# Experts on sorted tokens: 200 indirect transfers per image in place of dense expert products

## The chip, the cores and the metric

The kernel runs on one core of a Trainium2 chip. The time is the device time of one execution in microseconds (us), as the median of several executions. A profile is one further execution with every instruction recorded. Engines are named as in the profile: PE (TensorE, matmuls; PEld its weight loads), DVE (VectorE), ACT (ScalarE), POOL (GpSimd), SP (SyncE, which here only issues DMA transfers). Each engine works through its own instructions in program order and waits on semaphores of the others.

## The reference

Four images of 32 x 128 x 128 pass two layers. Layer 0 is an attention over blocks of channels; it enters here only as the work that layer 1 is interleaved with. Layer 1 turns the image into 4,096 rows ("tokens") of 128 numbers each (the sizes B, N in the functions below are not used), adds a linear attention, and then a mixture of experts:

```python
def _L1_ffn_ref(x, router_w, router_b, expert_w, expert_b):
    B, N, D, C, E, K = (8, 8192, 128, 128, 8, 2)
    router_probs = jax.nn.softmax(x @ router_w + router_b, axis=-1)
    top_p, top_i = jax.lax.top_k(router_probs, K)
    top_p = top_p / jnp.sum(top_p, axis=-1, keepdims=True)
    expert_out = jnp.einsum('bnd,edc->bnec', x, expert_w) + expert_b
    gathered = jnp.take_along_axis(expert_out, top_i[..., None], axis=2)
    return jnp.einsum('bnk,bnkc->bnc', top_p, gathered)
# ...
t = t + _L1_attn_ref(_ln_t(t), L1_attn_Wk, L1_attn_Wq, L1_attn_Wv)
t = t + _L1_ffn_ref(_ln_t(t), L1_ffn_router_w, L1_ffn_router_b, L1_ffn_expert_w, L1_ffn_expert_b)
```

Of the eight expert results of a token only the two with the highest router probability count. A kernel may compute all eight and weight six of them by zero, or compute two.

## The kernel before

The program is a loop over images. While the attention of image b is emitted, generators ("streams") are advanced between its instructions: the preparation of image b + 1 and layer 1 of image b - 1. A stream gets a begin, an end and a number of steps, in per cent of the attention's own units (`UNITS`); each `yield` of a generator is a step.

```python
    UNITS = 3 * NJ * NJ * NCH * (NCH - 1) // 2 + 5 * NJ * NCH
# ...
    for b in range(B):

        streams = list(carried)
        carried = []
        if b == 0:
            for kc, begin, end in ((1, 0, 5), (2, 6, 20), (3, 25, 45)):
                streams.append((prep(0, kc, states[0]), begin, end, 10))
            streams.append((setup_weights(), 50, 60, 4))
        else:
            streams.append((layer1(b - 1, states[b - 1], False), 7, 97, 161))
        if b + 1 < B:
            nxt = states[b + 1]
            streams.append((prep(b + 1, 0, nxt), 66, 84, 10))
            streams.append((prep(b + 1, 1, nxt), 85, 99, 10))
            carried.append((prep(b + 1, 2, nxt), 2, 20, 10))
            carried.append((prep(b + 1, 3, nxt), 30, 50, 10))
        done = [0] * len(streams)
        start = clock[0]
        for _ in attend(b, states[b]):
            t = 100 * (clock[0] - start) / UNITS
            for n, (steps, begin, end, count) in enumerate(streams):
                while t >= begin and done[n] * (end - begin) < (t - begin) * count:
                    next(steps, None)
                    done[n] += 1
        for steps, *_ in streams:
            for _ in steps:
                pass
    finish_late()
    last = states[B - 1]
    for _ in layer1(B - 1, last, True):
        pass
```

So layer 1 of images 0, 1 and 2 lies inside the attention of images 1, 2 and 3, and layer 1 of the last image stands alone at the end (`alone`). The attention itself, for each pair of chunks of tokens: a product on PE, its exponential on ACT, a product with the values on PE, and for the transposed half a block transpose on DVE (F), 16 transfers on SP that put the blocks together (G), and, `LAG` units later, products with G on PE:

```python
            for jc in order:
                if jc < i:
                    F = fpool.tile([P, 4, NJ, NJ, S], F32, tag="F", name=f"F_{b}_{i}_{jc}")
                    Fb = F.rearrange("p q ib j c -> p ib q j c")
                own = []
                # ...
                    nc.tensor.matmul(pe[:, c0:], qn[jc][:, ts(j, P)], qn[i][:, c0:], start=True, stop=True)
                    pr = ppool.tile([P, CH], F32, tag="pr", name=f"pr_{b}_{i}_{t}")
                    nc.scalar.activation(pr[:, c0:], pe[:, c0:], AF.Exp, accum_out=sums[:, t, i : i + 1])
                    # ...
                    if jc < i:
                        nc.vector.transpose(Fb[:, :, :, j, :], pr)
                    # ...
                if jc < i:
                    G = gpool.tile([P, 4, NJ, P], F32, tag="G", name=f"G_{b}_{i}_{jc}")
                    for a in range(4):
                        for q in range(4):
                            nc.sync.dma_start(
                                G[ts(q, S), a].rearrange("p ib f -> p (ib f)"),
                                F[ts(a, S), q].rearrange("p ib j c -> p (ib j c)"),
                            )
                    late.append((clock[0] + LAG, transposed_share(b, st, i, jc, G)))
# ... LAG = 56; fpool has 2 buffers, gpool 3. Later, from the G of that pair:
            nc.tensor.matmul(
                pg.rearrange("p (a f) -> p a f", a=4), st["qT"][i][:, ib, :], G[:, :, ib],
                start=(ib == 0), stop=(ib == NJ - 1),
            )
            junk = work.tile([P, 4, P], BF16, tag="junk", name=f"junk_{b}_{i}_{jc}_{ib}")
            nc.scalar.activation(
                junk, G[:, :, ib], AF.Copy, accum_out=st["sums"][:, NJ * i + ib, jc : jc + 1]
            )
```

Layer 1, as far as the change touches it: the tokens T are loaded by four transfers on SP, the attention of layer 0 is added, the rows are normalised (small powers on POOL), the linear attention is added, and the router's logits give one-hot vectors of the first and second expert. The weights of all experts go into `gate`, zero for six of eight:

```python
            nc.vector.tensor_tensor(o2, o2, mx.to_broadcast(sh), ALU.mult)
            nc.vector.tensor_tensor(o1, o1, o2, ALU.add)
            nc.vector.tensor_tensor(gate[:, rows], o1, dn.to_broadcast(sh), ALU.mult)
            yield
```

The experts are then dense: for every 128 tokens two products of 512 columns (four experts each), whose parts are scaled and added by DVE for one half of the experts and by ACT and POOL for the other:

```python
        for g in range(KT // 4):
            pb = psum_s(f"pbe_{b}_{g}")
            nc.tensor.matmul(pb, gates[g], ebd.rearrange("p j c -> p (j c)"), start=True, stop=True)
            acc = work.tile([P, 4, D], F32, tag="acc", name=f"acc_{b}_{g}", bufs=2)
            nc.vector.tensor_tensor(acc, T[:, ts(g, 4), :], pb.rearrange("p (j c) -> p j c", c=D), ALU.add)
            yield
            for jj in range(2):
                tmp = work.tile([P, 2, 4, D], F32, tag="wide", name=f"tmp_{b}_{g}_{jj}")
                for jk in range(2):
                    j = 2 * jj + jk
                    k = 4 * g + j
                    py = psum_y(f"py_{b}_{k}_0")
                    nc.tensor.matmul(py, xn[:, k, :], ew_sb[:, 0:4, :], start=True, stop=True)
                    for e in range(4):
                        nc.vector.scalar_tensor_tensor(
                            acc[:, j, :], py[:, ts(e, D)], gate[:, k, e : e + 1], acc[:, j, :], ALU.mult, ALU.add
                        )
                    yield
                    py = psum_y(f"py_{b}_{k}_1")
                    nc.tensor.matmul(py, xn[:, k, :], ew_sb[:, 4:8, :], start=True, stop=True)
                    for e in range(4):
                        nc.scalar.activation(
                            tmp[:, jk, e, :], py[:, ts(e, D)], AF.Copy, scale=gate[:, k, 4 + e : 5 + e]
                        )
                    yield
                nc.gpsimd.tensor_tensor(tmp[:, :, 0:2], tmp[:, :, 0:2], tmp[:, :, 2:4], ALU.add)
                nc.gpsimd.tensor_tensor(tmp[:, :, 0], tmp[:, :, 0], tmp[:, :, 1], ALU.add)
                if jj == 0 and g + 1 < KT // 4:
                    transpose_gate(g + 1)
                rows = acc[:, 2 * jj : 2 * jj + 2, :]
                nc.gpsimd.tensor_tensor(rows, rows, tmp[:, :, 0], ALU.add)
            for s in range(2):
                for r1 in range(2):
                    p0 = s * 64 + r1 * 32
                    nc.sync.dma_start(dst[s, r1, :, ts(g, 4), :], acc[p0 : p0 + 32])
```

## Time and profile before

| | |
|---|---|
| time, median of 3 | 1889.39 us (1889.33 to 1890.09) |
| span of the profiled execution | 1886.6 us |
| granted PE clock, mean | 0.983 of full speed |
| busy: PE, PEld, DVE, ACT, POOL | 1799.0, 915.4, 909.5, 974.6, 293.7 us |
| data moved by DMA | 145.68 MB, mean 77 GB/s |
| transfers issued on SP | 1,792 G, 64 xx, 16 T, 128 out |

The page gives the busy time of each engine, the span in 40 slices, the chain of work that ended last, and groups of instructions by line. A row of a group reads: line, engine, operation, what it writes <- what it reads, shape, count | busy us in total, mean ns of one | idle time of the engine just before, and what ended it. The span has four image periods and a tail; a period in the middle is about 453 us, from 836 to 1289 us for instance, in which the attention of image 2 and layer 1 of image 1 run together. From about 1720 us on only layer 1 of the last image is left. The costliest groups belong to the attention:

| group | count | busy us, mean ns |
|---|---|---|
| L244 PE po<-pr,qT (all shapes) | 1,152 | 551.1, 561 |
| L276 PE pe<-qn,qn 512 columns | 896 | 459.7, 595 |
| L213 PE pg<-G,qT 512 columns | 896 | 440.8, 594 |
| L278 ACT pr<-pe | 576 | 322.7, 560 |
| L285 DVE F<-pr | 448 | 311.4, 704 |

### The profile page before, as it was taken

To read this page: it belongs to the slowest core of one execution; us is meant where nothing else is said; L and a number is where in the kernel's file an instruction comes from. 1 tells how busy PE (TensorE), PEld (TensorE's weight loads), DVE (VectorE), ACT (ScalarE), POOL (GpSimd) and SP (SyncE) were. 2 spreads that over 40 slices of the span, in tenths; PEclk is the share of its full clock that TensorE was granted. 3 is DMA by queue.
4 is the path that set the end of the run, shared out by engine and by line. 5 is a ranking of instruction groups with operands and counts; after the bars stand their busy time and mean duration, and the time that the engine had idled before them with its cause. 6 is when DMAs were issued, how large, how long until landed. Compare 5 with 4: busy or idle time off the path is not lost.

```text
span 1886.6 us, 21105 instructions
## 1 busy us (share of the span) xinstructions
PE 1799.0 (95%) x5474; PEld 915.4 (49%) x5474; DVE 909.5 (48%) x2201; ACT 974.6 (52%) x3117; POOL 293.7 (16%) x279
## 2 busy tenths in 40 slices
PE   6999999998999999999999999999899999999678
PEld 4444544454555444455555444445465544444533
DVE  3343224345364454636355455453536445554576
ACT  3454444446457454555556655454554755554455
POOL 0000000002010122212000022220300012221336
PEclk9999999999999999999999999999999999999789
DMA  5333343332233232342233323234233223335001
GB/s 119 80 84 87 78 104 91 89 89 64 61 95 83 65 89 65 86 105 64 64 85 81 92 62 90 68 88 99 53 79 81 72 63 92 81 74 119 1 11 34
DMA packets 142247, 145.68 MB, mean 77 GB/s; under 512 B 32528, under 2 KB 84784, under 8 KB 142128
## 3 DMA queue, kind: packets, MB, share of 16 engines
q1 hardware_dynamic: 138496, 142.73, 31.5%
q10 hardware_dynamic: 3632, 1.60, 0.4%
q8 instruction: 45, 0.74, 0.2%
q14 instruction: 74, 0.61, 0.1%
HBM read 18.38 MB, written 8.39 MB: 14 GB/s over the span
## 4 chain that ended last, share of the span: by engine, by line
PE 81%; DVE 7%; SPq 4%; POOL 3%; ACT 2%; DMA 1%; issue 1%; ACTq 0%; POOLq 0%; DVEq 0%
PE po L244 23%; PE pe L276 20%; PE pg L213 18%; PE py L588 5%; PE py L581 5%; SPq L299 4%; PE pbe L571 1%; PE pat L468 1%; PE pgram L413 1%; DVE F L285 1%; PE ptd L255 1%; POOL rsa L111 1%; DVE df L387 1%; POOL T L395 1%; PE ptn L199 1%
## 5 line engine op out<-in xcount | busy, mean ns | idle before, releaser
L278 ACT ACTIVATE pr<-pe 128x512 f32<-128x512 f32 (+1 forms) x576 | 322.7, 560 | 519.6 <-PE pe L276 513.9
L244 PE MATMUL po<-pr,qT 128*128 128x512 f32 (+3 forms) x1152 | 551.1, 561 | 16.4 <-ACT pr L278 11.6
L285 DVE STREAM_TRANSPOSE F<-pr 128x512 f32<-128x512 f32 x448 | 311.4, 704 | 354.0 <-ACT pr L278 336.5
L276 PE MATMUL pe<-qn,qn 128*128 128x512 f32 x896 | 459.7, 595 | 0.0
L213 PE MATMUL pg<-G,qT 128*128 128x512 f32 x896 | 440.8, 594 | 1.7 <-DVE o L223 1.6
L244 PEld LDWEIGHTS po<-pr,qT 128*128 128x128 f32 x1152 | 213.3, 191 | 249.0 <-issue 182.9
L218 ACT ACTIVATE junk<-G 128x512 bf16<-128x512 f32 x448 | 277.1, 626 | 3.6 <-DMA G<-F 2.8
L213 PEld LDWEIGHTS pg<-G,qT 128*128 128x128 f32 x896 | 167.4, 191 | 196.0 <-issue 186.8
L590 ACT ACTIVATE tmp<-py,gate 128x128 f32<-128x128 f32 x512 | 146.3, 368 | 172.1 <-PE py L588 171.1
L583 DVE SCALAR_TENSOR_TENSOR acc<-py,gate,acc 128x128 f32<-128x128 f32 x512 | 177.7, 349 | 118.3 <-PE py L581 104.6
L276 PEld LDWEIGHTS pe<-qn,qn 128*128 128x128 f32 x896 | 160.9, 191 | 145.3 <-issue 144.4
L223 DVE TENSOR_TENSOR o<-o,pg 128x512 f32<-128x512 f32 x112 | 76.6, 684 | 184.4 <-PE pg L213 183.7
L594 POOL TENSOR_TENSOR tmp<-tmp 128x512 f32<-128x512 f32 x64 | 81.2, 1269 | 534.6 <-ACT tmp L590 534.6
L581 PE MATMUL py<-ew_sb,xn 128*128 128x512 f32 x256 | 132.7, 601 | 1.9 <-ACT tmp L590 1.2
L588 PE MATMUL py<-ew_sb,xn 128*128 128x512 f32 x256 | 131.9, 597 | 2.2 <-DVE acc L583 1.4
L278 ACT ACTIVATION_READ_ACCUMULATOR pr<-pe 128x1 f32 x576 | 114.5, 199 | 0.0
L111 POOL TENSOR_TENSOR rn<-ss,neg_half 128x8 f32<-128x8 f32 x16 | 26.2, 1639 | 500.4 <-DVE ss L185 500.4
L276 PE MATMUL pe<-qn 128*128 128x512 f32 (+3 forms) x256 | 90.3, 444 | 0.0
L218 ACT ACTIVATION_READ_ACCUMULATOR junk<-G 128x1 f32 x448 | 88.5, 198 | 0.0
L370 ACT ACTIVATE xn<-T,nba,rsa 128x128 f32<-128x128 f32 x128 | 51.9, 481 | 55.1 <-DVE nba L367 55.1
L111 POOL TENSOR_TENSOR rsf<-dm_f,neg_half 128x8 f32<-128x8 f32 x16 | 26.3, 1642 | 342.5 <-DVE dm_f L365 342.5
L588 PEld LDWEIGHTS py<-ew_sb,xn 128*128 128x128 f32 x256 | 48.5, 191 | 61.9 <-issue 53.0
(121 smaller groups left out, 1416.5 us busy)
## 6 DMA issues: line engine op xcount, KB each, us to landing
G<-F SPq DMA_DIRECT2D x1792, 64.0 KB, 2.0
xx<-in_x_dram SPq DMA_DIRECT2D x64, 128.0 KB, 2.8
T<-in_x_dram SPq DMA_DIRECT2D x16, 512.0 KB, 7.1
out_dram<-acc SPq DMA_DIRECT2D x128, 64.0 KB, 1.8
ew_sb<-in_L_ffn_expert_w_dram ACTq DMA_DIRECT2D x1, 512.0 KB, 5.4
raw_w<-in_L_attn_Wv_dram ACTq DMA_DIRECT2D x1, 512.0 KB
raw_w<-in_L_attn_Wk_dram ACTq DMA_DIRECT2D x1, 256.0 KB
raw_w<-in_L_attn_Wq_dram ACTq DMA_DIRECT2D x1, 256.0 KB
```

Source lines behind the costliest of these rows:

```text
L213: nc.tensor.matmul(pg.rearrange("p (a f) -> p a f", a=4), st["qT"][i][:, ib, :], G[:, :, ib], start=(ib == 0), stop=(ib == NJ - 1),)
L218: nc.scalar.activation(junk, G[:, :, ib], AF.Copy, accum_out=st["sums"][:, NJ * i + ib, jc : jc + 1])
L223: nc.vector.tensor_tensor(o, o, pg.rearrange("p (a j c) -> p a j c", a=4, c=S), ALU.add)
L244: nc.tensor.matmul(po[:, lo:hi], qT[blk // NJ][:, blk % NJ, :], w, start=(count[0] == 1), stop=(count[0] == total))
L276: nc.tensor.matmul(pe[:, c0:], qn[jc][:, ts(j, P)], qn[i][:, c0:], start=True, stop=True)
L278: nc.scalar.activation(pr[:, c0:], pe[:, c0:], AF.Exp, accum_out=sums[:, t, i : i + 1])
L285: nc.vector.transpose(Fb[:, :, :, j, :], pr)
L581: nc.tensor.matmul(py, xn[:, k, :], ew_sb[:, 0:4, :], start=True, stop=True)
L583: nc.vector.scalar_tensor_tensor(acc[:, j, :], py[:, ts(e, D)], gate[:, k, e : e + 1], acc[:, j, :], ALU.mult, ALU.add)
L588: nc.tensor.matmul(py, xn[:, k, :], ew_sb[:, 4:8, :], start=True, stop=True)
L590: nc.scalar.activation(tmp[:, jk, e, :], py[:, ts(e, D)], AF.Copy, scale=gate[:, k, 4 + e : 5 + e])
L594: nc.gpsimd.tensor_tensor(tmp[:, :, 0:2], tmp[:, :, 0:2], tmp[:, :, 2:4], ALU.add)
```

## The change

For the first three images the dense experts are replaced by sorted ones. Every token has two pairs (token, expert). Prefix sums over the one-hot vectors and two small matmuls give each pair a place in a list that is sorted by expert, each expert's part rounded up to tiles of 128 places (72 tiles in all, `NT`). Then: the normalised rows are scattered to their places in DRAM (64 indirect transfers of 128 rows), each tile is loaded back, transposed and multiplied by the weights of its one expert, which are gathered by row numbers from a table in DRAM (72 indirect transfers, 128 rows of weights and bias, 1 KB each); results are stored to DRAM, and for each token its two rows are gathered back (64 indirect transfers) and added with their weights. Indirect transfers are issued by POOL. The list in DRAM is filled first with rows of x, so that unused places hold numbers. It is meant to save the six products of eight that are weighted by zero. The last image keeps the dense form.

The diff, cut (`# ...` marks a cut):

```diff
+    NT = 2 * KT + E
# ... constants: below, ones, upto, tiles_of, tile_no, part_no; table = [E * D, 2 * D] in DRAM
+        rows = table.rearrange("(e d) c -> d e c", e=E)
+        nc.scalar.dma_start(rows[:, :, :D], ew_sb)
+        bias = work.tile([P, E, D], F32, tag="wide", name="bias_rows")
+        nc.scalar.dma_start(bias, expert_b.partition_broadcast(P))
+        nc.scalar.dma_start(rows[:, :, D:], bias)
# ...
+    def sorted_experts(b, st, T, xn, first, second, weight, psum_s):
# ... runs over tokens, pairs per expert, place of each pair (7 steps)
+        pc = psum_s(f"pcnt_{b}")
+        nc.tensor.matmul(pc[:, :E], below, run[:, KT - 1, :], start=True, stop=True)
+        nc.tensor.matmul(pc[:, E : 2 * E], ones, run[:, KT - 1, :], start=True, stop=True)
# ... owner of each tile, row numbers of its weights
+        scatters = []
+        for k in range(KT):
+            for n in range(2):
+                inst = nc.gpsimd.indirect_dma_start(xs, offset(place[:, n, k : k + 1]), xn[:, k, :], None)
+                if scatters:
+                    tc.declare_no_dep(inst.ins, group=f"scatter_{b}", reason="no two tokens have the same place")
+                tc.add_to_no_dep_group(f"scatter_{b}", inst.ins)
+                after(inst.ins, st["fills"], "the place was filled before")
+                scatters.append(inst.ins)
+            yield
+        buf = big1.tile([P, 8, 4, D], F32, tag="xn", name=f"ffn_{b}")
+        wts = {}
+
+        def load(g):
+            rows_g = xs[ts(g, 4 * P), :].rearrange("(j p) d -> p j d", p=P)
+            inst = nc.sync.dma_start(buf[:, g % 3], rows_g)
+            after(inst.ins, scatters, "a tile holds tokens of any row")
+
+        def weights(g):
+            wts[g] = work.tile([P, 4, 2 * D], F32, tag="wide", name=f"wt_{b}_{g}")
+            for j in range(4):
+                t = 4 * g + j
+                nc.gpsimd.indirect_dma_start(wts[g][:, j, :], None, table, offset(rows[:, t : t + 1]))
+
+        def turn_rows(g):
+            pt = psum_s(f"pts_{b}_{g}")
+            for j in range(4):
+                nc.tensor.transpose(pt[:, ts(j, P)], buf[:, g % 3, j, :], ident)
+            nc.scalar.activation(buf[:, 3 + g % 2], pt.rearrange("p (j t) -> p j t", t=P), AF.Copy)
+
+        def apply(g):
+            py = ps_y.tile([P, CH], F32, tag="py", name=f"pys_{b}_{g}")
+            for j in range(4):
+                nc.tensor.matmul(py[:, ts(j, D)], buf[:, 3 + g % 2, j, :], wts[g][:, j, :D], start=True, stop=True)
+            yt = buf[:, 5 + g % 2]
+            nc.vector.tensor_tensor(yt, py.rearrange("p (j c) -> p j c", c=D), wts[g][:, :, D:], ALU.add)
+            nc.sync.dma_start(ys[ts(g, 4 * P), :].rearrange("(j p) d -> p j d", p=P), yt)
+
+        NG = NT // 4
+        for g in range(NG + 8):
+            if 5 <= g < NG + 5:
+                load(g - 5)
+            if 6 <= g < NG + 6:
+                weights(g - 6)
+            yield
+            if 7 <= g < NG + 7:
+                turn_rows(g - 7)
+            yield
+            if 8 <= g:
+                apply(g - 8)
+            yield
+
+        dst = tokens(out, b)
+        accs = {}
+        for g in range(KT // 4 + 1):
+            if g < KT // 4:
+                accs[g] = work.tile([P, 4, D], F32, tag="acc", name=f"acc_{b}_{g}", bufs=2)
+                for j in range(4):
+                    k = 4 * g + j
+                    nc.gpsimd.indirect_dma_start(accs[g][:, j, :], None, ys, offset(place[:, 0, k : k + 1]))
+                    nc.gpsimd.indirect_dma_start(buf[:, g % 3, j, :], None, ys, offset(place[:, 1, k : k + 1]))
+                    yield
+            if g >= 1:
+                g -= 1
+                acc = accs[g]
+                for j in range(4):
+                    k = 4 * g + j
+                    nc.vector.scalar_tensor_tensor(
+                        acc[:, j, :], acc[:, j, :], weight[:, 0, k, :], T[:, k, :], ALU.mult, ALU.add
+                    )
+                    nc.vector.scalar_tensor_tensor(
+                        acc[:, j, :], buf[:, g % 3, j, :], weight[:, 1, k, :], acc[:, j, :], ALU.mult, ALU.add
+                    )
+                    if j == 1:
+                        yield
+                for s in range(2):
+                    for r1 in range(2):
+                        p0 = s * 64 + r1 * 32
+                        nc.sync.dma_start(dst[s, r1, :, ts(g, 4), :], acc[p0 : p0 + 32])
+                yield
+
# ... in layer1, while the attention of layer 0 is divided:
+        def fill(g):
+
+            rows = x[b].rearrange("c h w -> (c h) w")
+            at = g * 4 * P % rows.shape[0]
+            inst = nc.sync.dma_start(st["xs"][ts(g, 4 * P), :], rows[at : at + 4 * P, :])
+            st.setdefault("fills", []).append(inst.ins)
+                if not alone:
+                    for g in range(3 * (2 * kc + s), min(3 * (2 * kc + s) + 3, NT // 4)):
+                        fill(g)
# ... the normalised rows stay in xn; after the routing:
-        for u in range(6):
+        for u in range(6 if alone else 5):
+            if not alone and 0 <= u - 1:
+                for k in range(8 * u - 8, 8 * u):
+                    normalise(xn[:, k, :], k, rsf, nbf)
+                yield
+            for g in (2 * u - 4, 2 * u - 3) if alone else ():
                 if 0 <= g - 1:
+        if not alone:
+            yield from sorted_experts(b, st, T, xn, first, second, weight, psum_t)
+            return
# ...
+            streams.append((setup_sorting(), 40, 50, 3))
-            streams.append((layer1(b - 1, states[b - 1], False), 7, 97, 161))
+            streams.append((layer1(b - 1, states[b - 1], False), 7, 97, 240))
```

Beside this, `gate` and the one-hot vectors move between pools, `wts` and `owner` share the two buffers of the tag "wide", `buf` (tiles loaded, transposed, results) takes the place of xn once the scatters have read it, and layer 1 of the first three images now has 240 steps in place of 161 over the same share of the attention (7% to 97%).

## The prediction

> **What bounds the kernel now.** I read the page's busy times first, then the busy time by stretches, the chain of waits for true matmul rates, and last the waits and the timeline of the SyncE DMA queue, because the change puts most of its new work on queues.
>
> ```profile
> PE 1799.0 (95%) x5474; PEld 915.4 (49%) x5474; DVE 909.5 (48%) x2201; ACT 974.6 (52%) x3117; POOL 293.7 (16%) x279
> ...
> PEclk9999999999999999999999999999999999999789
> DMA  5333343332233232342233323234233223335001
> ```
>
> TensorE is busy nearly throughout, its clock is granted, every other engine is half idle. For one whole image period in the middle (836 to 1289 us; the first row is the period, the others are parts of it):
>
> ```profile
> core 0: us, PE busy (x) PEld busy (x) DVE busy (x) ACT busy (x) POOL busy (x), PEclk, DMA share, GB/s
> 836.00:1289.00 453.00, 445.56 (x1363) 226.78 (x1362) 227.17 (x548) 243.09 (x784) 73.53 (x66) 0.99 0.33 80
> 881.00:926.00 45.00, 39.67 (x139) 23.00 (x138) 20.58 (x55) 28.35 (x87) 9.63 (x5) 0.89 0.21 52
> 1061.00:1106.00 45.00, 45.00 (x127) 21.83 (x126) 18.48 (x39) 23.85 (x80) 5.45 (x6) 1.00 0.25 62
> ```
>
> 445.6 of 453 us: in the stretch in which one image's attention covers the layer 1 of the image before, TensorE is the bound, and only 881 to 926 us has holes. So a microsecond of matmul removed there is a microsecond of the end, if nothing takes its place. The rows of what is removed:
>
> ```profile
> L583 DVE SCALAR_TENSOR_TENSOR acc<-py,gate,acc 128x128 f32<-128x128 f32 x512 | 177.7, 349 | 118.3 <-PE py L581 104.6
> L581 PE MATMUL py<-ew_sb,xn 128*128 128x512 f32 x256 | 132.7, 601 | 1.9 <-ACT tmp L590 1.2
> L588 PE MATMUL py<-ew_sb,xn 128*128 128x512 f32 x256 | 131.9, 597 | 2.2 <-DVE acc L583 1.4
> ```
>
> The 600 ns are not what one costs. The chain of waits (start, length, work) gives the rate back to back:
>
> ```profile
> 854.15 3.43 PE pg L213 x8
> ...
> 916.38 1.79 PE pgram L413 x16
> ```
>
> 8 instructions of 512 columns in 3.43 us: 0.429 us each. 16 of 128 columns in 1.79 us: 0.112 us each. The timeline has four transposes of 128 columns (ptf) in 0.60 us, the last of them 0.285 long: 0.105 us each. An fp32 matmul is two instructions, a transpose one.
>
> The queue that moves the data is less free than the DMA share of 0.33 suggests. Its waits in the same period, and its timeline at the start of it:
>
> ```profile
> SPq L299 <- DVE F L285: 101.8, 16, 17.0
> SPq L603 <- POOL acc L599: 29.1, 6, 15.2
> ```
> ```profile
> 860.57 67.97 SPq L299 DMA_DIRECT2D G<-F  x64
> 928.59 0.58 SPq L157 DMA_DIRECT2D xx<-in_x_dram  x1
> 932.72 20.68 SPq L299 DMA_DIRECT2D G<-F  x32
> ```
>
> SyncE waits about 137 of 453 us (these two and 6 us of small ones), so it issues for 316 us; about 500 transfers make 0.63 us each. Just after the four T loads 64 take 68 us, over 1 us each: SyncE is the busiest issuer and is in order, so whatever blocks it also holds the G tiles that TensorE needs.
>
> **What the Trainium skill says.** *Perfetto Trace Analysis*, "Identifying the Most-Contended Engine", warns that matmul busy time overstates, since matmuls are pipelined. This trace agrees: 601 ns on the row, 429 in the chain. *DMA: Bandwidth & Descriptors*, "SWDGE vs HWDGE vs iDMA": for DMAs issued from GpSimd, indirect ones included, a Q7 core computes the descriptors in software; its "Latency and other measured facts" gives about 1 us to the first byte. The kernel before has no such DMA, so no trace here shows its cost. The same page, "Issuing engines are not separate DMA queues": all queues end on the same 16 engines. *SBUF — State Buffer*, "Who interferes with whom": a VectorE instruction with two SBUF inputs contends with a GpSimd instruction that reads SBUF. The trace before cannot test the last two for indirect DMAs.
>
> **The change part by part, per sorted image.**
>
> *TensorE.* Removed: 128 expert instructions x 0.429 = 54.9; 16 of the bias product (pbe) x 0.429 = 6.9; 8 gate and 32 token transposes x 0.105 = 4.2; together 66.0 us. Added: 72 tiles (64 full by 8,192 token-expert pairs, up to 8 more by rounding up per expert), each a transpose, 72 x 0.105 = 7.6, and a matmul of two instructions, 144 x 0.112 = 16.1; two small count products 0.4; together 24.1. Net -41.9 us, and for three images -126 us: 1889.4 - 126 = 1764 us, if TensorE stays the bound. The last image is dense in both, so the tail should stay.
>
> *ScalarE and VectorE.* ScalarE loses 128 scalings (36.6 us) and 8 evictions x 0.595 (4.8), and gains 18 evictions x 0.59 (10.6): -31. VectorE loses 44.6 (L583), 5.5 (L573), 2.3 (gT); it gains 64 combining instructions at an estimated 0.28 (the rate of a 128-wide SBUF row such as the 280 ns of BATCH_NORM) = 18, 18 bias adds x 0.69 = 12.4, and about 25 small sorting instructions, 10 us: -12. Neither was the bound.
>
> *SyncE and the 16 DMA engines.* 18 fills, 18 loads and 18 stores: 54 x 0.55 = 30 us more issue, 346 of a period near 411. It fits if nothing blocks it. Data packets: now 34,816 in 453 us at a share of 0.328, so 68 ns each with the semaphore packets and 2 KB G packets among them. The T load shows short packets alone: 4 x 1,024 of 512 B, landing after 10.1 us, 39 ns each on 16 engines. The change adds per image up to 9,216 for fills, 8,192 for scatters, 9,216 each for loads, weights and stores, 8,192 for gathers, 53,000 in all: x 39 / 16 = 130 us, 32% of the period. DMA share 0.36 + 0.32, about 0.68. Not full, but the G transfers (median 2.0 us) will queue. The fills are the worst: 18 in the first part of layer 1, in the stretch where SyncE is solid. I charge 4 us per image for this.
>
> *GpSimd.* It loses 44 us of tmp and acc adds and gains 64 scatters, 72 weight gathers and 64 result gathers: 200 indirect DMAs per image. Their cost, c, is the number I do not have. What it may be follows from the pacing. The layer takes 240 steps over 90% of an image's units, so a step is 0.375%. The attention's own matmuls, counted with the rates above, are about 338 us per image, so a step is 1.27 us plus the layer's own matmuls in it. Counting steps: scatters begin at step 80 and the first load, which waits for all of them, is at 127 (weights at 130); 50 x 1.28 = 64 us for 64 DMAs. Weights and tiles, 54 steps and 24 us of tile matmuls: 93 us for 72. Result gathers, 48 steps: 61 us for 64, less some 4 us, since the first waits until the last results have landed. So GpSimd keeps up only if c is about 1.0, 1.29 and 0.9 us in the three stages. Beyond that the in-order queues block: SyncE at the load, TensorE at a tile without weights, VectorE at the combination or at the rn power of the next image's preparation (GpSimd, behind the gathers). About 5 us per stage are absorbed by the distance of 56 units, some 13 us, between a G transfer and its use. What is left, per image: c = 1.0, about 4 us; 1.1, 14; 1.2, 23; 1.3, 36; 1.4, 57; 1.5, 77; then 20 more for each 0.1.
>
> **Sum.** My middle value for c is 1.15 us: the skill's about 1 us plus reading 128 offsets (an estimate). Lag about 17 us, DMA contention 4: -42 + 21 = -21 per image, -63 for three: 1826 us. Predicted 1825.
>
> **The rivals.**
>
> *GpSimd becomes the bound.* At c = 1.35 the lag eats the 42 us; at 1.5 the kernel takes 1889 + 3 x (77 + 4 - 42) = about 2006; at 2 about 2300. For it: 200 software-made DMAs per image on one queue and no slack in the pacing. Against it: GpSimd is busy only 73.5 of 453 us now, and the steps between the last scatter and the first load look like a distance set on purpose.
>
> *DMA contention or a blocked SyncE becomes the bound.* For it: 64 transfers in 68 us after a mere 2 MB of T, SyncE's 15.2 us wait for acc already now, 4.7 MB of fills at that very place. It would cost 10 to 20 us per image even at c = 1: 1795 to 1825. Against it: a share of 0.33 now, and 137 us of SyncE's waiting per period.
>
> *The full gain.* c at or under 1.0 and G transfers still in time: 1764 to 1785. For it: VectorE and ScalarE also get lighter, so their few blockings of TensorE (3.5 us for pr in the period) shrink.
>
> *The weights' two buffers as a wait.* The weight gather of group g waits for the tile product of group g - 2, which stands later in the same turn of the loop; 4c plus about 2 us landing must fit in six steps, about 9 us. That binds only from c about 1.6, where GpSimd is the bound already.
>
> **Range and chances.** c under 1.2 gives 1765 to 1840, to which I give a good half; 1.2 to 1.4 lands near the time before; above it the kernel is slower, quickly. 8 in 10: 1765 to 1975, skewed upward since lag has no ceiling and the gain has one. Faster by over 2% (under 1851.6): 0.52; within 2%: 0.18; slower: 0.30.
>
> **What would show each step right or wrong.** TensorE busy per middle image down by about 50 us on the rows' scale, py rows of the first three images gone, pts transposes and pys matmuls near 0.11 us each back to back: the first step. Spacing of scatters and gathers on GpSimd: c itself. SyncE's longest waits naming the scatters or the combination, and TensorE idle on weights, name the lag; TensorE idle on G with GpSimd idle would mean contention. DMA share near 0.68 checks the packets. The prediction is wrong if c is far from 1.15, if a GpSimd queue full of waiting DMAs also holds the small powers longer than counted, or if the sorted period shows new holes before its first scatter, which would be the fills.

## The result, and the profile after

| | before | after |
|---|---|---|
| time, median | 1889.65 us (1889.33 to 1890.09) | 2306.16 us (2304.15 to 2315.4) |
| ratio, 95% interval | | 1.221 (1.218 to 1.225) |
| period of a middle image | 453 us | 562 us (1005 to 1567 us, from one T load to the next) |
| data moved by DMA | 145.68 MB | 243.30 MB |

The kernel is 22% slower; 1825 us was predicted. The page of the changed kernel, the same three rows that were read of before:

```profile
PE 1809.3 (78%) x5582; PEld 929.0 (40%) x5582; DVE 848.1 (37%) x2095; ACT 888.7 (39%) x2763; POOL 736.0 (32%) x737
...
PEclk9999999999669987899976989799997599968789
DMA  6333334445226644342422565335232256534301
```

TensorE has fallen from 95% to 78%, ScalarE and VectorE do less than before, and no engine has become the bound: GpSimd is busy for a third of the time. So time is lost in holes in which nobody works. The granted clock shows where: one deep dip for each sorted image, at its scatters, and a shallower one later, at its result gathers. The second deep one by stretches of 16 us:

```profile
core 0: us, PE busy (x) PEld busy (x) DVE busy (x) ACT busy (x) POOL busy (x), PEclk, DMA share, GB/s
1144.00:1160.00 16.00, 15.29 (x49) 7.72 (x47) 5.51 (x18) 6.67 (x26) 9.56 (x10) 1.00 0.37 106
1160.00:1176.00 16.00, 3.68 (x4) 1.14 (x4) 1.35 (x2) 1.30 (x4) 12.04 (x14) 0.70 0.15 49
1176.00:1192.00 16.00, 7.95 (x9) 3.00 (x10) 1.42 (x2) 0.76 (x3) 12.34 (x13) 0.61 0.40 111
1192.00:1208.00 16.00, 7.79 (x16) 3.02 (x14) 0.71 (x1) 3.13 (x10) 12.04 (x14) 0.82 0.20 63
1208.00:1224.00 16.00, 3.78 (x4) 1.17 (x4) 0.71 (x1) 0.69 (x2) 12.21 (x13) 0.50 0.15 50
1224.00:1240.00 16.00, 0.00 (x0) 0.00 (x0) 0.69 (x1) 0.00 (x0) 11.54 (x12) 0.50 0.28 80
1256.00:1272.00 16.00, 16.00 (x42) 7.34 (x41) 4.87 (x7) 9.78 (x30) 0.00 (x0) 1.00 0.42 102
```

From 1160 to 1240 us GpSimd alone keeps working, 12 of every 16 us, and it issues indirect transfers; TensorE is busy for 0 to 8 of 16. The DMA engines are mostly emptier than in the period before the change (0.15 to 0.40, against 0.33 there), so this is not a full memory system. The granted clock falls after TensorE has gone idle (TensorE stops at 1159.3 us, the clock is 0.50 from 1162.9), and comes back with it. What GpSimd does, and who waits:

```profile
L450 POOL DMA_INDIRECT wt<-table,rows x216 | 206.0, 954 | 368.4 <-DVE ffn L463 207.3
L431 POOL DMA_INDIRECT xs<-xn,place x192 | 184.9, 963 | 83.6 <-issue 53.6
```
```profile
ACT pr L314 <- PE pe L312: 545.2, 320, 8.6
ACT pr L314 <- remote: 248.8, 30, 29.2
PE po L280 <- ACT pr L314: 237.0, 46, 34.7
```

An indirect transfer occupies GpSimd for 0.96 us, and the next starts 0.3 us later: 64 scatters from 1149.0 to 1229.3 us, 1.27 us each. In the list of waits (total, times, longest) "remote" is what the profile calls a wait whose release no engine's record explains: 30 times ScalarE stood like that, up to 29 us, before an exponential; the one that starts at 1187.1 us has its scores, by TensorE's record, since 1179.9. TensorE then stands for ScalarE, up to 35 us. Nobody waits for a scatter, and SyncE's list has no wait on one. The holes are not the lag that the prediction computed: in that, TensorE or SyncE would stand at a tile load.

### The profile page after: what moved, and what is told of

Same layout as the page of the kernel before. It is cut to its first block, busy times and chain, and to the rows that moved or that the text cites. A ratio compares the mean times of both kernels' runs of the same rounds, so it can differ in the third digit from the quotient of the medians.

```text
span 2306.0 us, 22018 instructions
## 1 busy us (share of the span) xinstructions
PE 1809.3 (78%) x5582; PEld 929.0 (40%) x5582; DVE 848.1 (37%) x2095; ACT 888.7 (39%) x2763; POOL 736.0 (32%) x737
## 2 busy tenths in 40 slices
DMA packets 225885, 243.30 MB, mean 106 GB/s; under 512 B 44768, under 2 KB 154368, under 8 KB 224896
## 3 DMA queue, kind: packets, MB, share of 16 engines
q1 hardware_dynamic: 197248, 185.21, 30.8%
q0 software_dynamic: 22656, 53.52, 8.4%
## 5 line engine op out<-in xcount | busy, mean ns | idle before, releaser
L280 PE MATMUL po<-pr,qT 128*128 128x512 f32 (+3 forms) x1152 | 594.8, 601 | 338.9 <-ACT pr L314 237.0
L312 PE MATMUL pe<-qn,qn 128*128 128x512 f32 x896 | 489.4, 629 | 0.0
L450 POOL DMA_INDIRECT wt<-table,rows x216 | 206.0, 954 | 368.4 <-DVE ffn L463 207.3
L312 PEld LDWEIGHTS pe<-qn,qn 128*128 128x128 f32 x896 | 170.1, 203 | 153.4 <-issue 152.7
L431 POOL DMA_INDIRECT xs<-xn,place x192 | 184.9, 963 | 83.6 <-issue 53.6
L461 PE MATMUL pys<-wt,ffn 128*128 128x128 f32 x432 | 82.2, 309 | 45.9 <-DMA wt<-table,rows 32.1
L487 POOL DMA_INDIRECT acc<-ys,place x96 | 90.9, 947 | 78.8 <-issue 49.0
L488 POOL DMA_INDIRECT ffn<-ys,place x96 | 91.8, 957 | 68.7 <-DVE acc L495 31.6
L461 PEld LDWEIGHTS pys<-wt,ffn 128*128 128x128 f32 x432 | 66.0, 204 | 91.6 <-issue 47.5
L463 DVE TENSOR_TENSOR ffn<-pys,wt 128x512 f32<-128x512 f32 x54 | 36.6, 678 | 116.1 <-PE pys L461 49.3
```

Source lines behind the costliest of these rows:

```text
L280: nc.tensor.matmul(po[:, lo:hi], qT[blk // NJ][:, blk % NJ, :], w, start=(count[0] == 1), stop=(count[0] == total))
L431: inst = nc.gpsimd.indirect_dma_start(xs, offset(place[:, n, k : k + 1]), xn[:, k, :], None)
L450: nc.gpsimd.indirect_dma_start(wts[g][:, j, :], None, table, offset(rows[:, t : t + 1]))
L461: nc.tensor.matmul(py[:, ts(j, D)], buf[:, 3 + g % 2, j, :], wts[g][:, j, :D], start=True, stop=True)
L487: nc.gpsimd.indirect_dma_start(accs[g][:, j, :], None, ys, offset(place[:, 0, k : k + 1]))
L488: nc.gpsimd.indirect_dma_start(buf[:, g % 3, j, :], None, ys, offset(place[:, 1, k : k + 1]))
```

## The experiments

The theory after these readings, A: GpSimd's indirect transfers, issued back to back, slow other engines that have nothing to do with them. Rival B: GpSimd's chain is late for the program, and the others wait in order. Rival C: the DMA traffic does it. Rival D: the throttle does it. (The expectations, quoted as they stood before each run, name their theories anew.)

**1. Which transfers carry the loss.** Four kernels leave parts out. Without scatters, or with plain ones, the tiles hold whatever lies in the rows, so no tokens are sorted; for weight gathers the resident weights of some expert stand in; without result gathers the output is combined from a buffer.

```diff
  no_scatter:     - for n in range(2):          + for n in range(0):
  scatter_plain:  - nc.gpsimd.indirect_dma_start(xs, offset(place[:, n, k : k + 1]), xn[:, k, :], None)
                  + nc.gpsimd.dma_start(xs[ts(2 * k + n, P), :], xn[:, k, :])
  no_indirect:    no scatters; wts[g] = ew_sb (resident); results combined from buf, no gathers
  no_scatter_no_weights: no scatters; wts[g] = ew_sb; result gathers kept
```

> The changed kernel with its 200 indirect transfers per sorted image left out (tiles are loaded from the fills, weights come from the resident experts, results are combined from what lies in the buffer). All else of the change stays, so its time shows the matmuls saved and the cost of the 54 plain transfers. Both theories: 1764 if the matmul sum of the prediction holds and the transfers hide, up to 1790 with contention. If it stays over 1850, the sum itself was wrong.

> The changed kernel without the 64 scatters per image alone (tiles are loaded from the fills); weight gathers and result gathers stay. Theory A: the holes at the scatters, about 66 us per image by the busy time of TensorE (29 of 96 us), vanish: about 2306 - 200 = 2106 us. Theory B, with the lag counted in the prediction at 1.27 us per transfer: the scatter stage lags 82 - 64 = 18 us per image at most: about 2250 us.

> The scatters replaced by plain GpSimd transfers of the same rows to 128 places in a row: same count, bytes, queue, waits; no row numbers. Theory A with row numbers as the cause: the holes vanish, about 2106 us. Theory A with any GpSimd transfer as the cause: they stay, near 2306. Theory B: the stage changes only by the difference in the cost of one transfer on GpSimd (1.27 us now).

> Leaves out scatters and weight gathers (resident weights of some expert instead), keeps the 64 result gathers of each sorted image. With 2069 us without scatters and 1841 us without any indirect transfer, 228 us belong to 72 weight gathers and 64 result gathers of each of three images. Theory A (a starved TensorE, 0.67 us for each transfer issued back to back, plus what waits for them): result gathers come in one run of 64, the weight gathers in fours with pauses for the engine behind, so the results take the larger part: 1960 to 2000 us here. Rival: the weights' two buffers make GpSimd and TensorE wait for one another and take the larger part: 1870 to 1920 us.

Measured: without indirect transfers 1840.7 us, 51 above the expected range (ratio to before 0.975, 0.973 to 0.976); without scatters 2069.1 (1.094, 1.091 to 1.098); scatters as plain transfers of the same bytes on the same queue 2072.7 (1.098, 1.096 to 1.099); without scatters and weight gathers 1976.4 (1.046, 1.044 to 1.047). The second and third are nearer to A's 2106 us than to B's 2250, the last lies in A's range.

So of 465 us between 2306 and 1841, taken out in this order, the 192 scatters carry 237, the 216 weight gathers 93, the 192 result gathers 136. The bytes are not it: as plain transfers, with the same 225,885 packets in the whole kernel, the scatters cost 4 us more than none at all, which is within the spread of the runs. That ends rival C for the scatters. It does not end B: a plain transfer costs GpSimd 0.54 us, an indirect one 1.27, and a plain one need not wait for the row numbers. It starts when its rows are normalised, at 491.7 us in the first sorted image, where the change starts at 565.3. The scatter stage of the kernel with plain transfers, beside the same stage of the changed one:

```profile
core 0: us, PE busy (x) PEld busy (x) DVE busy (x) ACT busy (x) POOL busy (x), PEclk, DMA share, GB/s
996.00:1053.00 57.00, 55.17 (x192) 29.75 (x191) 38.01 (x135) 37.04 (x114) 39.35 (x67) 1.00 0.60 177
```
```profile
1149.00:1230.00 81.00, 33.48 (x62) 13.06 (x60) 5.67 (x8) 10.48 (x34) 61.79 (x64) 0.69 0.24 73
```

**2. TensorE alone beside transfers that it does not depend on.** Stages of 200 fp32 matmuls of 512 columns (400 passes of weight load and matmul) on resident data, and on GpSimd 64 transfers with no dependency to them. The first such kernel also had stages in which TensorE and ScalarE hand tiles to each other.

```diff
+ free_pe("a")
+ scatter("b"); free_pe("b")      # then gathers (c), 1 KB gathers (d), plain on GpSimd (e), on SyncE (f); hand-over stages g to l
```

> A kernel of stages and nothing else: TensorE runs the same fp32 products of 512 columns (200 of them into one bank, or 100 that hand over to ScalarE and back), while GpSimd or SyncE issues 64 or 72 transfers that depend on nothing TensorE does; stages are alone, scatter, gather of 512 B rows, gather of 1 KB rows, plain GpSimd writes, plain SyncE writes. Theory A (the scatters slow TensorE itself, whatever waits for what): a stage of 200 products takes 172 us alone and 50 us or more longer beside 64 scatters, and beside the plain SyncE writes it stays at 172. Theory B (the loss is program order: something waits for a GpSimd queue that lags): all stages without a wait between the two engines take 172 us within 5. Theory C (only the hand-over of a finished product is late, not the products): the 200 products take 172 us in every stage, the hand-over stages get longer beside scatters.

From the start of the first matmul to the start of the last, the passes take 174.0 us alone (the first stage of the program), 171.3 beside plain transfers on GpSimd or SyncE, 214.2 beside 64 scatters, 215.3 beside gathers, 226.3 beside 72 gathers of 1 KB rows. The loss beside scatters is 43 us, a little under A's 50. The 64 plain transfers of GpSimd are over in 34 us, too soon to tell much; the second kernel has 192. With the hand-over the loss is larger (229 to 240 against 171). TensorE's rows and a piece of its timeline in the scatter stage:

```profile
L87 PE MATMUL acc_a<-mov,sta x400: 592/592/1192, 3.7 to 177.7; 128*128 128x512 f32 x134
...
L87 PE MATMUL acc_b<-mov,sta x400: 589/592/1117, 179.8 to 394.0; 128*128 128x512 f32 x134
```
```profile
225.02 1.01 PE L87 MATMUL acc_b<-mov,sta 128*128 128x512 f32 x1 [2.21 <-issue]
227.82 1.01 PE L87 MATMUL acc_b<-mov,sta 128*128 128x512 f32 x1 [1.79 <-issue]
230.62 1.01 PE L87 MATMUL acc_b<-mov,sta 128*128 128x512 f32 x1 [1.79 <-issue]
```

For 39 us after GpSimd begins nothing happens, then TensorE starts one pass every 2.80 us instead of every 0.43, until GpSimd ends. "issue" says that it waits for nothing the profile shows. No dependency, no hand-over, no data are needed: 0.67 us of TensorE for each indirect transfer on average (42.9 us over 64), so B is not the whole story. It stays open what runs dry. A second kernel varies the passes, the engine and the number of transfers.

```diff
+ short_pe: matmuls of 128 columns x800;  bf_pe: bf16, 512 columns x700
+ act_stream, dve_stream: 250 operations of 512 columns on ScalarE, on VectorE
+ plain_long: 192 plain GpSimd transfers;  scatter(n=16), scatter(n=32);  busy_pool: 64 multiplies
```

> Stages of TensorE, ScalarE or VectorE streams, each alone and then beside scatters on GpSimd; nothing of the reference is computed. Theory A (TensorE's instruction supply starves while GpSimd issues indirect transfers: one pass per about 2.80 us whatever its size, after a buffered stretch of about 91 passes): 128-column passes (four times shorter) also come one per 2.8 us once 91 passes are used up, after about 10 us instead of 39, so this stage, of the same columns in all, loses about 65 to 75 us and not 42; bf16 passes likewise. 16 scatters (20 us) beside 512-column passes cost nothing, 32 (41 us) next to nothing. ScalarE and VectorE may show the same rhythm if their supply is shared. 192 plain transfers on GpSimd (over 100 us) cost TensorE nothing if it is the row numbers; they slow it if any long run of GpSimd transfers does. Theory B (operands: the moving data is read 6.5 times more slowly per column): 128-column passes come one per 0.7 us, the loss begins at once or after the same 39 us, and this stage loses as much as the 512-column one (42 us); 16 scatters cost about 11 us. Theory C (the throttle): the granted clock falls before the passes slow. Scatters with a GpSimd memset after each: A expects a smaller loss per scatter, or none, if the supply refills in the gaps; a fixed 0.67 us per scatter keeps the loss at 42 us. 64 GpSimd multiplies without transfers: no loss, unless GpSimd's work itself takes ports.

Passes of 128 columns, four times shorter, also come one per 2.8 us (7 in 20 us); the first gaps stand after 10 us already, and the stage takes 256 us instead of 179, a loss of 77 us. The bf16 stage goes from 151 to 215. The stretch at full rate is some 90 to 100 passes in each, whatever their size. So it is instructions, not operands, that come slowly. 192 plain transfers over 102 us cost TensorE nothing (600 passes in 257 us), 64 multiplies on GpSimd nothing. The granted clock follows: in the first kernel the passes come slowly from 219.4 us on and the clock stays at 1.00 until 224.1, here the two times are 542.4 and 545.5 us. D falls. The scatters of 16 and 32 followed one another and so made a run of 60 us, which cost 25 us; the two stages that were to have memsets between the scatters got them ahead of the stage instead, and lost the 43 us of a dense run. ScalarE and VectorE:

```profile
core 0: us, PE busy (x) PEld busy (x) DVE busy (x) ACT busy (x) POOL busy (x), PEclk, DMA share, GB/s
1420.00:1440.00 20.00, 20.00 (x48) 8.91 (x47) 0.00 (x0) 19.02 (x32) 15.15 (x16) 1.00 0.15 53
1460.00:1480.00 20.00, 7.31 (x8) 2.02 (x7) 0.00 (x0) 9.22 (x15) 15.13 (x17) 0.50 0.14 49
1560.00:1580.00 20.00, 20.00 (x48) 8.80 (x47) 19.05 (x29) 0.00 (x0) 15.99 (x14) 1.00 0.13 46
```

In the second row TensorE (7 weight loads and 8 matmuls in 20 us) and ScalarE (15 operations) are slow together, in the same run of scatters that left both alone 30 us earlier (first row): each engine gets one instruction per 1.40 us (a pass is two; in the timeline ScalarE's operations start 1.40 us apart). In the third row VectorE is streaming, the scatters come 1.45 us apart (not 1.40, as the later expectations have it), and TensorE runs at its full rate. This was not foreseen, and leads to the next question: is it VectorE, or the distance of the transfers?

The whole kernel has another rhythm. In its scatter stage from 1149 us on, exponentials start 11 to 13 us apart (1162.1, 1175.4, 1187.1, 1198.7, 1210.6), each 3 to 9 us after its scores were done, while eight matmuls on one G in between took only 4.7 us. How passes of 2.80 us add up to such rounds, when the engines wait for one another, no run shows.

The third kernel varies the distance:

```diff
  for k in range(0, n, burst):
+     gi = work.tile([P, 1024], U32, tag=f"gi{bufs}", name=f"gi_{stage}_{k}", bufs=bufs)
+     nc.gpsimd.tensor_copy(gi[:, :w], big[:, k : k + w])     # then `burst` scatters by columns of gi
```

> Stages of 200 fp32 matmuls of 512 columns (250 in stage e) beside 64 scatters on GpSimd; nothing of the reference is computed. Alone 172 us, beside scatters back to back about 215 us. In the run before, the scatters that lay beside a stream of VectorE operations came 1.40 us apart instead of 1.27, and TensorE lost nothing. Theory A (what counts is how closely GpSimd's indirect transfers follow one another; a little air between them lets the instruction supply of the others keep up): a GpSimd copy of the row numbers ahead of each scatter, of 1, 64 or 256 columns, brings the loss from 43 us to under 15 us, and to nothing for the longer copies. Pauses after every 8 or 16 scatters (each wait for the landing, 2 to 3 us) leave most of the loss if the pause must be as long as the refill, and take it away if the buffered stretch refills quickly. Theory B (it was VectorE's activity itself, holding GpSimd off some port, and not the spacing): all paced stages keep most of the loss, 0.6 us or so for each scatter, unless VectorE runs. Theory C (each indirect transfer costs the supply a fixed time whatever its spacing): the loss stays 0.67 us for each of the 64 scatters, 43 us, in all stages.

```profile
L87 PE MATMUL acc_b<-mov,sta x400: 589/592/1107, 179.2 to 393.6; 128*128 128x512 f32 x134
...
L87 PE MATMUL acc_c<-mov,sta x400: 592/592/697, 394.8 to 566.2; 128*128 128x512 f32 x134
...
L87 PE MATMUL acc_g<-mov,sta x400: 592/592/697, 1174.2 to 1345.6; 128*128 128x512 f32 x134
...
L87 PE MATMUL acc_h<-mov,sta x400: 589/592/1061, 1346.9 to 1544.8; 128*128 128x512 f32 x134
```

Dense scatters (b, 1.27 us apart) 214.4 us. A one-column copy of 0.19 us ahead of each (c, 1.47 us) 171.4, no loss; longer copies the same. A wait for the landing after every 8 (g, 1.47 on average) 171.4; after every 16 (h, 1.35) 197.9; a copy ahead of every 4 (1.29) 217. It is the distance. The edge lies between 1.35 us (with pauses after every 16) and 1.45 us (beside VectorE), not far above the 1.27 us that GpSimd needs by itself; no even distance in between was run.

What runs dry is not settled. The transfers of the trace's instruction queue, 16 KB each, took 0.9 to 1.5 us, also the few that fall into slow stretches (0.92 us at 567 us in the stage of short passes), so no late block is to be seen. The Trainium skill, *Runtime: NRT & Kernel Launch*, "Instruction fetch mechanics", describes just such 16 KB blocks, fetched ahead by each engine; that much agrees, but no run here shows the way from the block to the engine.

**3. Pace in the whole kernel.** The same copy ahead of every transfer of the changed kernel (the memory left room for eight columns), and ahead of the scatters only:

```diff
+ turned = stat.tile([P, 8], U32, tag="turned", name=f"turned_{b}", bufs=1)
+ def paced(ap):
+     at = turned[:, len(taken) % 8 : len(taken) % 8 + 1]    # paced_2: % 2
+     taken.append(at)
+     nc.gpsimd.tensor_copy(at, ap)
+     return offset(at)
- nc.gpsimd.indirect_dma_start(xs, offset(place[:, n, k : k + 1]), xn[:, k, :], None)
+ nc.gpsimd.indirect_dma_start(xs, paced(place[:, n, k : k + 1]), xn[:, k, :], None)   # and so for both gathers
```

> The changed kernel, whole, but every indirect transfer takes its row numbers from a one-column copy that GpSimd makes shortly before it (about 0.19 us each, 200 for each sorted image), so that the transfers follow one another at 1.45 to 1.5 us on average instead of 1.25 to 1.27. Theory A (transfers that follow too closely starve the instruction supply of TensorE and ScalarE; with a little air they don't): the idle holes of 60 to 70 us in each scatter stage go, TensorE's busy share rises, and the time falls from 2306 us to 1860 to 1930 us: the 1841 us of no indirect transfer at all plus what GpSimd's 200 x 1.47 us leave visible. Rival (GpSimd as the bound: its chain of transfers sets the period, and making it longer by 200 x 0.2 us makes it worse): 2306 + 3 x 40 = about 2430 us.

> As before, but only the 64 scatters of each sorted image are paced by a copy; weight and result gathers stay back to back. Without scatters at all the kernel took 2069 us. Theory A: 2060 to 2110 us, as if the scatters were not there. Rival (GpSimd bound): 2306 + 3 x 13 = about 2345 us.

2268.3 us (1.199, 1.195 to 1.203) and 2258.3 (1.194, 1.192 to 1.197): both misses, by over 300 and nearly 150 us. The instructions stood in fours, four copies and four transfers, 1.27 us apart three times and then 1.65: 1.37 on average where nothing else held them, hardly above what still lost time in the stages, and the holes were still there. With two columns, copies and transfers alternate:

> The changed kernel, whole, with each indirect transfer's row numbers copied by GpSimd just before it, as before, but now through two columns in turn, so that copy and transfer alternate strictly and a copy waits until the transfer two before it has landed. The first paced kernel put its copies in fours, its transfers came 1.27 us apart three times and then 1.65 us, 1.365 us on average, and the holes stayed. In the stages by themselves 1.35 us still lost 26 us of 43, and 1.40 us and 1.47 us lost nothing. Theory A (too close a succession starves the others): spacing becomes 1.5 us or more, the holes in the scatter stages go, and the time is 1841 us plus what a longer chain on GpSimd costs, 1880 to 2000 us. Rival (GpSimd's chain is the bound and the holes only follow from waiting for it): longer than paced, 2300 us or more.

2244.4 us (1.188, 1.186 to 1.190), again a miss, and an instructive one. The second scatter stage by stretches, and TensorE and SyncE at its end:

```profile
core 0: us, PE busy (x) PEld busy (x) DVE busy (x) ACT busy (x) POOL busy (x), PEclk, DMA share, GB/s
1148.00:1180.00 32.00, 32.00 (x82) 14.62 (x81) 9.91 (x15) 16.43 (x50) 21.52 (x39) 1.00 0.53 140
1196.00:1240.00 44.00, 3.94 (x7) 1.07 (x5) 0.69 (x1) 2.56 (x8) 32.78 (x57) 0.54 0.22 65
```
```profile
1240.31 1.11 PE L464 MATMUL pts<-ident,ffn 128*128 128x128 f32 x4 [36.65 <-DMA ffn<-xs]
```
```profile
1198.93 0.59 SPq L193 DMA_DIRECT2D xx<-in_x_dram  x1
1236.77 1.48 SPq L452 DMA_DIRECT2D ffn<-xs  x3
```

For the first 60 us TensorE is busy with hardly a gap beside the scatters (A is right about the cause). Then it stands 36.7 us at the transposes of the first tile, whose load has to wait for the last scatter, and SyncE stands before that load from 1199.5 to 1236.8 us with every other transfer behind it. That is the prediction's lag, word for word, and rival B: 64 scatters at 1.6 us are 101 us, the prediction counted 64 us of the program for them, and it is less (part 4). Pace trades one loss for the other. Three more kernels look for a way between: one ties each transfer to the attention's latest exponential, so that GpSimd cannot run ahead; one has the copy (three columns) and more room in the program; one the room without the copy.

```diff
  tied:      + after(inst.ins, [latest[0]], "no further ahead than the attention");  one scatter to a step
  spread_3:  + 81 steps in 7..28%, then one transfer to a step up to 99%; xs shared and filled once; paced, % 3
  spread_0:  as spread_3 without paced()
```

> The changed kernel, whole, without copies, but each indirect transfer waits for the latest exponential of the attention at its place in the program, and there is one scatter to a step instead of two, so that GpSimd can't run ahead of TensorE. Theory A: whenever TensorE starves GpSimd has to wait for it, so transfers come at TensorE's pace and the starved stretches end by themselves: well under the 2306 us of the change, 1900 to 2050 us. Rival (TensorE waits for results of GpSimd): tying GpSimd to ScalarE adds waits and gives 2306 us or more.

> The changed kernel, whole, with both causes treated at once: each indirect transfer takes its row numbers from a GpSimd copy made just before it, through three columns in turn (about 1.47 us from one transfer to the next), and the program gives the 200 transfers of an image 71% of the image's attention instead of about 57% (first 81 steps of the layer in 21%, then one transfer to a step, about 1.5 us each). The places are filled once, for the first image only. The strictly paced kernel before ran its scatters at 1.54 us beside a TensorE at its full rate, until TensorE and SyncE stood 37 us at the first tile load, which waits for the last scatter: the program had left the 64 scatters too little time. Theory (back to back the transfers starve the other engines, paced they are late for the program; with pace and room neither happens): 1850 to 1930 us, perhaps below the 1889 us of the kernel before. Rival (something else about 200 indirect transfers holds TensorE): 2100 us or more.

> The same program order, room and single filling as the run beside it, but without the copies: the transfers may follow one another as closely as GpSimd issues them. Theory: GpSimd is ready early, issues at 1.27 us, and starves TensorE and ScalarE in each of its long runs; the holes stay: 2050 to 2250 us. Rival (only the room in the program mattered, not the pace): the same as the paced one, within 40 us.

2202.1 us (1.165, 1.162 to 1.168), 2184.7 (1.158, 1.156 to 1.160) and 2320.6 (1.228, 1.226 to 1.230). All three miss the theory. Room alone brings nothing (spread_0 is 14 us slower than the change), pace with it brings 121 us, not the 376 or more that were expected: 2184.7 us lies in the range of the rival, that something else holds TensorE. In the scatter stage of spread_3 (1075 to 1180 us) TensorE was busy for 74 of 105 us with the transfers 1.46 us apart (1.52 with their stops), and ScalarE still stood up to 12 us for a "remote" release, so the starving is smaller there but not gone. VectorE waited 17 us at one place for the small power `rn`, which GpSimd computes in order behind the scatters, and TensorE then 9 us for VectorE. No kernel that sorts beat the one before.

**4. How the 465 us split.** Plain transfers need no row numbers and starve nobody; with other GpSimd work ahead of each, GpSimd's chain is as long as with indirect ones. What is then left above 1841 us was meant to be lateness.

```diff
  scatters:  + nc.gpsimd.tensor_scalar(xn[:, k, :], xn[:, k, :], 1.0, None, ALU.mult)      # twice, and a copy
             + nc.gpsimd.dma_start(xs[ts(2 * k + n, P), :], xn[:, k, :])
  weights:   + 3 x nc.gpsimd.memset(wts[g][:, j, :], 0.0);  nc.gpsimd.dma_start(wts[g][:, j, :], table[ts(t % E, P), :])
  results:   + 4 x nc.gpsimd.memset(...);  nc.gpsimd.dma_start(..., ys[ts(...), :])
```

(Rows go to fixed places and fixed rows come back, so nothing is sorted; scatter_plain_slow changes the scatters only, all_plain_127 has a copy of one column and one memset fewer.)

> The changed kernel with its 64 scatters of each image replaced by plain GpSimd transfers of the same rows to fixed places (tokens are not sorted), and with GpSimd operations on each row block ahead of them, so that GpSimd's chain is as long as with the scatters (0.54 us a transfer and about 0.7 us of other work). Without that work the plain transfers took 2073 us. Theory A (row numbers starve the others; GpSimd's time isn't the point in this stage): 2060 to 2130 us, and TensorE busy through the stage. Rival (the stage stands because 64 times 1.27 us on GpSimd are late for the program): close to the 2306 us of the change, 2230 us or more.

> As the run beside it, with the 72 weight gathers and the 64 result gathers also replaced by plain GpSimd transfers of fixed rows, each behind fills of its destination, so that all 200 transfers of an image cost GpSimd about what the indirect ones do (near 1.27 us), without a row number anywhere. It splits the 465 us between 1841 us (nothing indirect) and 2306 us: what is left above 1841 us here is the lateness of GpSimd's chain, what is missing below 2306 us is the starving of the others by indirect transfers. Theory A: lateness as the table of the prediction has it for 1.27 us, about 30 us an image, 1900 to 1960 us. Rival (lateness is most of it): 2150 us or more.

> As the run with all 200 transfers plain behind other GpSimd work (2045 us), but with less of that work, so that a transfer costs GpSimd 1.25 to 1.3 us, as the indirect ones do, and not 1.3 to 1.5. That run stands 204 us above the kernel without indirect transfers, 68 us an image, where the table of the prediction has 77 us for 1.5 us a transfer. If the table's steepness is right too (30 us an image at 1.27, some 20 us for each 0.1), this one takes about 1930 us, 1900 to 1970, and of the 465 us some 90 are lateness and 375 starvation. If lateness does not depend so much on the pace (waits of SyncE and VectorE for the plain transfers as such), it stays at 2000 us or more, and starvation is some 260 to 300 us.

2083.6 us (1.103, 1.101 to 1.105), in A's range: making the plain transfers as slow as, or slower than, the indirect ones (1.47 us each) costs 11 us over scatter_plain, and is still 222 us faster than the change, though TensorE was busy for 66.7 of 94 us only. All three stages: 2045.4 (1.082, 1.079 to 1.084) with scatters at 1.47, between theory and rival, and 2012.9 (1.066, 1.064 to 1.068) with scatters at 1.35, not the 1900 to 1970 of the theory. The page of the last, and two waits that grew:

```profile
PE 1749.1 (87%) x5582; PEld 910.2 (45%) x5582; DVE 857.8 (43%) x2095; ACT 890.5 (44%) x2763; POOL 887.5 (44%) x2387
```
```profile
DVE nbf L568 <- POOL rsf L149: 77.9, 16, 9.8
ACT xn L571 <- DVE nbf L568: 69.6, 12, 9.9
```

GpSimd is busier than in the changed kernel (887.5 us against 736.0) and the kernel 293 us faster. That looks like a split, 172 us of lateness and 293 for the row numbers, but it is none. A plain transfer does not wait for its row numbers: in the first sorted image of all_plain_127 the scatters stand at 491.9 to 576.2 us and are over before the row numbers (`place`) are complete. And the work ahead of them holds up the small powers of the normalisation (the two waits above), so that `place` is complete at 593.6 us, where the change has it at 565.0. From there to the first tile load it takes 57 us, as long as in the kernel without indirect transfers. These kernels have no late scatters at all, and a late routing that the change does not have.

For the scatter stage a split can be read from two kernels that are alike up to the row numbers, the change (first rows) and no_indirect. SyncE in the second sorted image:

```profile
1109.28 171.57 SPq L335 DMA_DIRECT2D G<-F  x128
1281.17 0.94 SPq L443 DMA_DIRECT2D ffn<-xs  x2
```
```profile
955.68 93.41 SPq L335 DMA_DIRECT2D G<-F  x128
1049.13 1.15 SPq L443 DMA_DIRECT2D ffn<-xs  x2
```

`place` is complete at 1147.9 us here and at 994.3 there, in both 39 us after the first of these rows begins. The first tile load (second row) follows `place` by 55 us without indirect transfers and by 133 us in the change; in the three images it is 56, 55 and 57 us against 136, 133 and 137. The differences are 238 us in all, just what leaving out the scatters brings (237). The chain of scatters allows the load 82 to 84 us after `place`: the last scatter is issued after 80 to 81 us, and in paced_2 the load follows the last scatter by 2.4 us. So at most 25 to 29 us an image, 81 in all, are lateness, rival B. The other 157 us, about 52 an image, are not: the scatters are done, and SyncE is still at the attention's shares G, which took 172 us instead of 93, behind engines that stood. In paced_2, the same program with the scatters further apart, this second part is missing (the load comes 103 to 105 us after `place`, right behind the last scatter). For the weight and result gathers, 93 and 136 us, no run gives such a split.

**5. Where 77 us went that are missing even without indirect transfers** (1841, where the sum has 1764):

```diff
  no_indirect_no_fill:     - fill(g);  load(g) reads the image's own rows
  no_indirect_pool_queue:  - nc.sync.dma_start(...)   + nc.gpsimd.dma_start(...)   # fills, tile loads, ys stores, out stores
```

> Leaves out all indirect transfers and the 18 fills of each sorted image (14 MB in and 14 MB out in all); the tiles are loaded from the image's own rows, in any order, so no tokens are sorted. Theory: without indirect transfers the sorting stages still gain only 48 us instead of the 126 of the sum because the fills collide with the load of T and the turned shares G. If so, this comes out at 1775 to 1800 us. Rival: the missing gain is work of the added stages in the order of the program (waits on VectorE and SyncE for the combination, the tile loads), not the fills: then 1825 to 1841 us.

> As the kernel without indirect transfers (1841 us; weights, row order and combination are not the reference's), with the fills, tile loads, result stores and output stores of the sorted images issued by GpSimd, which is nearly idle there, instead of SyncE. Theory: what keeps that kernel from the 1764 us of the sum is SyncE's in-order queue (12% of its chain against 4% before): with about 86 issues of 0.55 us fewer in each period the turned shares G start earlier; 1795 to 1820 us. Rival (the transfers themselves, or short matmuls that cost TensorE more than the 0.11 us each that was counted): 1835 us or more.

1838.3 us (0.973, 0.972 to 0.975): the fills cost nothing that can be told. 1807.2 (0.957, 0.956 to 0.959): taking the sorted images' transfers out of SyncE's queue brings 34 us. The chain that ended last, without and with that:

```profile
PE 68%; SPq 12%; DVE 9%; POOL 3%; DMA 3%; issue 2%; ACT 2%; ACTq 0%; POOLq 0%; DVEq 0%
```
```profile
PE 68%; DVE 9%; DMA 7%; SPq 6%; POOL 5%; issue 3%; ACT 2%; ACTq 0%; POOLq 0%; DVEq 0%
```

Before the change SyncE's queue had 4% of this chain and TensorE 81%. With less work on TensorE between two chunks of attention, the 16 issues of each G, about 10 us of SyncE, have less to hide behind. The other 43 us are not settled. One candidate is in the rows of the kernel without indirect transfers: 432 pys matmuls were busy 57.4 us and 216 pts transposes 32.5, together 90 us where the sum counted 71. Part of that may be apparent only, since the busy time of a short group contains the tail of its last instruction; no run tests it.

## Why the prediction was wrong

**The step that failed** is in the GpSimd part: "200 indirect DMAs per image. Their cost, c, is the number I do not have." It charged c to GpSimd alone, and let the others pay only by waiting for its results. No step, and no rival, had TensorE and ScalarE run slower while GpSimd issues. What the runs showed in its place: alone beside 64 scatters, with nothing to wait for, TensorE takes 214 us in place of 171, 0.67 us more for each transfer; and of the 238 us that the three scatter stages lose in the kernel, about 157 are of this kind and at most 81 are the lateness that the prediction reckoned with. From 1841 us without indirect transfers, 237 for the scatters, 93 for the weight gathers and 136 for the result gathers lead to the 2306; how much of the last two is starving is not known.

**c itself** was near: 1.25 to 1.27 us against the middle value of 1.15, one tenth beyond, well inside the table. That was luck in part: the prediction took a time to the first byte for the time that GpSimd spends on a transfer. Measured are 0.96 us busy and 0.3 us until the next one.

**The lag table** has the right mechanism (paced_2 shows SyncE at the load and TensorE at the tile, as written). Its count of the scatter stage was somewhat generous: it gives the 64 scatters 64 us of the program, and without indirect transfers it is 55 to 57. At 1.27 us a transfer they are up to 25 to 29 us late per image, where the count gives 17, before the 5 us that are absorbed. The rest of the table is not tested, not by the plain transfers either, as these do not start where the indirect ones do.

**TensorE's sum** of -42 us an image: without indirect transfers TensorE's busy time fell by 96 us in all (1799.0 to 1702.9) and the time by 49, not 126. The py rows of the first three images are gone and the tail stayed, as said.

**DMA and SyncE.** "The fills are the worst ... I charge 4 us per image": the fills cost nothing measurable, but SyncE's queue as such cost 34 us, 11 an image, in the range that the rival gave it (10 to 20). The DMA share came to 0.44 in a period without indirect transfers, and to 0.40 in the changed kernel (30.8%, 8.4% and 0.5% of its queues), not 0.68: the change added 27,900 packets an image (225,885 against 142,247), not 53,000; the 600 indirect transfers came as 22,656 packets, about 38 each and not 128. Lighter traffic did not help, since it was not the limit.

**ScalarE and VectorE** fell by 29 and 20 us an image (predicted 31 and 12); neither mattered.

**The rivals.** "GpSimd becomes the bound" had the sign, but by its own table 1.27 us gives about 1870 us. That the table has about 2300 us at c = 2, close to what was measured, is chance: c was 1.27, and GpSimd was busy for a third of the time. The two that spoke for the gain have a part in the kernel without indirect transfers, and none in the change. The weights' two buffers: GpSimd's 207 us of waiting for the tile product (`wt <- ffn`) were there in the change and in all_plain_127 alike, so they are not what tells the two apart.

**The chances.** 0.52 for faster came from c alone. A kind of transfer that no trace of the kernel before contains called for a wider range upward, since nothing was known of what it does to the others.

## What to carry to other kernels

An engine that issues work of a new kind can slow engines with which it shares no tile and no queue: before 600 of them go into a kernel, put a handful of stages on the chip in which each engine streams alone beside it. When all engines are idle at once and only GpSimd issues, look at the distance from one indirect transfer to the next, not at the DMA share; a short copy ahead of each (1.47 us apart) or a wait after every eight was enough beside TensorE alone, and in the scatter stage of the whole kernel 1.6 us was, where 1.46 was not quite. The program must also have the room that this takes. In this kernel none of the tried ways had it, and dense products without row numbers were the better bargain.

## What the hardware showed that was not expected

- Indirect transfers 1.27 us apart let TensorE start one pass (weight load and matmul) per 2.80 us, be it of 512 or 128 columns, fp32 or bf16, and ScalarE one operation per 1.40 us; plain transfers 0.54 us apart on the same queue, 192 in a row, let TensorE run freely.
- The slow rhythm begins only after some 90 to 100 passes on TensorE, 39 us of 512-column fp32 or 10 us of 128-column passes, and ends within some 10 us of the last transfer.
- The edge is sharp: 1.27 and 1.29 us apart cost 43 to 46 us of a 171 us stage, 1.35 costs 26, 1.45 and 1.47 nothing. In the whole kernel something was still lost at 1.46.
- VectorE's two-input stream pushed the scatters from 1.27 to 1.45 us apart, and TensorE beside them lost nothing.
- The granted clock fell to 0.50 in the slow stretches, as a consequence: beside the first scatters of TensorE alone it fell 4.7 us after the passes had become slow.
